# Four edits in the last attention layer: the next norm, the output rows, the row sums and the last 64 rows' product

## The chip, the cores and the metric

The kernel runs on one core of one Trainium2 chip. The metric is the device time of one launch in microseconds (us), less is better. The engines of a core are called PE (TensorE, matmuls; its weight loads are listed apart), DVE (VectorE), ACT (ScalarE), POOL (GpSimd) and SP, whose queue issues all loads and stores of this part of the kernel. Each engine runs its instructions in the order in which the program issued them and waits on semaphores for the others.

## The reference, cut to what matters

Four layers run on x (8 batches of 100 rows of 512 channels) with a context of 361 rows for each batch, all in fp32. The change is in the last layer alone: two cross-attentions, each behind a layer norm, and an MLP.

```python
def _cross_attention(q_in, kv_in, wq, bq, wk, bk, wv, bv, wo, bo, bias_k, bias_v):
    qh = (q_in @ wq + bq).reshape(b, q_len, H, K)            # 16 heads of 128
    kh, vh = kv_in @ wk + bk, kv_in @ wv + bv                # one more key and value
    ...                                                      # per head: bias_k, bias_v
    weights = softmax(einsum('bqhk,bthk->bhqt', qh, kh) / sqrt(K))
    ctx = einsum('bhqt,bthk->bqhk', weights, vh).reshape(b, q_len, H * K)
    return ctx @ wo + bo

h = layer_norm(x, ln1_scale, ln1_offset)
x = x + _cross_attention(h, context, ... first weights ...)
h = layer_norm(x, ln2_scale, ln2_offset)
x = x + _cross_attention(h, context, ... second weights ...)
h = layer_norm(x, ln_mlp_scale, ln_mlp_offset)
return x + gelu(h @ w_fc1 + b_fc1) @ w_fc2 + b_fc2
```

## The kernel before, in words

The last layer runs as four steps: attention 1 and 2, each for two halves of four batches (400 rows of x, 200 in `HN`). x itself lies in DRAM (`xd`): `take_rows` loads rows of it and `put_rows` stores them. A step has three parts.

*Queries* (`project_queries`). The normed rows stand in `hT`, turned (channels on partitions). `wq` is applied head by head, two heads at a time, as one 2x2 block product in seven multiplications instead of eight (`seven_products`), which needs sums of the weights' blocks (`left_sums`, on POOL) and of the tokens' blocks (`right_sums` into `hs`, four DVE instructions ahead of the first head pair). Each product is a matmul `pq`. Then `wk` is applied to the queries (`pk`), so that scores can be taken against the raw context: `qz` holds, per batch, 512 channels for 1600 rows (16 heads of 100). `some_keys` puts the `pk` of the head pair before between the products of this pair; in the first pair there is none before, and nothing is put there.

*Attention* (`attend`, once per batch). 1600 rows are 12 tiles of 128 (`NT`, `TR`) and 64 rows left over (`RR`). A tile pair's scores (`pair_of_scores`, 128x361 each in the banks `su` and `sl`) are again a block product in seven multiplications, with context sums `ts` once per batch and row sums `ss` once per pair, all on POOL. `softmax` follows on DVE and ACT, `turn_rows` turns the probabilities (`pt`, into `at`), and `block_with_context` multiplies four tiles by the context: weights are blocks of the context rows `cr` and their sums `cs`, with `at` moving, and the result overwrites `qz`. Products wait in the list `waiting`, and `meanwhile` takes parts of it, up to 256 rows' worth, between the products of a later pair: so PE's order is made. The 64 left rows of two batches are done together as one tile of 128: the scores (L1377) put the two batches' results in the two halves of a bank's partitions, and after the softmax `with_context` multiplies each batch's 64 rows: 4 channel blocks of 3 context blocks, each with weights `cr` 121x128 and 64 columns moving, 24 matmuls for the two batches. The results are channel by row, as `qz` has them.

*Outputs* (`project_outputs`). For each pair of heads: `wv` applied to `qz` (`pa`, L97 by its helper), the added key's part `u` (loaded from `pd`, L1443, then POOL), their sum `aT` (DVE, L1454), sums of `wo` (POOL) and the seven products `po` (L1416) of the pair before, which DVE adds to seven sums in SBUF, `acc` (L1425), of which three lie in the tile tag `oT` of the pool `big` and four in the tile `more` of the pool `l3_out`. The last pair ends with a few more adds (L1427). Then 16 transposes per step (L1466) turn the sums into rows, DVE adds them to x's rows (L1467) and `put_rows` stores these. `normalize` is called ahead of `project_outputs` and norms the rows of the *next* step (the other half, or after the second attention the MLP's first half): loads, `bn_stats`, `xhat` (L109), transposes (L128), and ACT's scale and offset into the next `hT`. Both loads of x's rows use the four buffers of tag `xin`.

Pools: `big` and `l3_2` stay for the layer, `l3_ctx` (context and its sums) is open in a step's queries and attention, `l3_out` in its outputs, in the same place. The MLP's first weights' second part is loaded into memory that `big` and others held (L1512), so that load waits for their last readers; the first part is loaded before the last outputs.

Of the kernel before, what the change touches and what calls it, by code (L numbers as in the profile page):

```python
# [10 lines left out]
F32 = mybir.dt.float32  # L11
# [45 lines left out]
def kernel(ctx: ExitStack, tc: tile.TileContext, d: dict, out: bass.AP):  # L57
# [1015 lines left out]
    with ExitStack() as es:  # L1073
# [85 lines left out]

        def project_queries(layer, hT, added):  # L1160
            ep, ahead = None, None
# [9 lines left out]

            b = [[hT[:, 2 * k : 2 * k + 2, n * HN : (n + 1) * HN] for n in range(2)] for k in range(2)]
            hs = big.tile([P, 4, 2, HN], F32, tag="oT", name="hs")
            hs = [hs[:, k] for k in range(4)]
            right_sums(nc.vector, b, hs)
            for h in range(0, NH, 2):
                wqs = [head_tile("wq", layer, h + m, "wa", [P, NC, P]) for m in range(2)]
                wks = [head_tile("wk", layer, h + m, "wb", [P, C]) for m in range(2)]
                a = [[w[:, 2 * k : 2 * k + 2, :] for k in range(2)] for w in wqs]
                s = p2.tile([P, 4, 2, TR], F32, tag="ss4", name="wqs").rearrange("p i k r -> p (i k r)")  # L1180
                s = [s[:, k * 2 * P : (k + 1) * 2 * P].rearrange("p (k m) -> p k m", k=2) for k in range(3)]
                left_sums(nc.gpsimd, a, s)
                banks = [ps.tile([P, 512], F32, tag=g, name=n) for g, n in (("z", "pq"), ("mm", "pq"))]
                tu = p2.tile([P, 3, HN], F32, tag="xhat", name="tu")
                if h == 10:
                    ep = added_scores(hT, er, *added)
# [23 lines left out]

        def attend(b, i, ep, pd, waiting, turning, pc, loaded):

# [4 lines left out]
            nc.sync.dma_start(out=cr, in_=d["ctxR"][b])  # L1217
            loaded.append((cT, cr))


# [7 lines left out]


            bs = [[cT[:, 2 * k : 2 * k + 2, j * SH : (j + 1) * SH] for j in range(2)] for k in range(2)]  # L1230
            ts_ = pc.tile([P, 4, 2, SH], F32, tag="ts", name="ts", bufs=1)
            nc.gpsimd.tensor_tensor(ts_[:, 0], bs[0][1], bs[0][0], ALU.subtract)
            nc.gpsimd.tensor_tensor(ts_[:, 1], bs[1][1], ts_[:, 0], ALU.subtract)  # L1233
            nc.gpsimd.tensor_tensor(ts_[:, 2], bs[1][1], bs[0][1], ALU.subtract)
            nc.gpsimd.tensor_tensor(ts_[:, 3], bs[1][0], ts_[:, 1], ALU.subtract)

            def sums(t):

# [7 lines left out]

            def with_context(i, cr, cs, at, r0):
                n = at.shape[-1]
                pz = ps.tile([P, 512], F32, tag="z", name="pz")
                pz = pz[:, : 2 * n].rearrange("p (c n) -> p c n", c=2)  # L1250
                for k, c in enumerate(cs):
                    mm_sum(
                        pz[:, k],
                        [
                            (cr[:m, kb, c * P : (c + 1) * P], at[:m, kb])
                            for kb, m in enumerate((KB, KB, S - 2 * KB))
                        ],
                    )
                evict(qz[:, i, cs[0] : cs[0] + 2, r0 : r0 + n], pz)

# [11 lines left out]
            def pair_of_scores(t):  # L1272
                rows, s = sums(t)
                banks = [ps.tile([P, 512], F32, tag=g, name=n)[:TR] for g, n in (("sc", "su"), ("mm", "sl"))]
                tu = p2.tile([P, 3, HN], F32, tag="xhat", name="tu")[:TR, :, :SH]

                def first():
# [7 lines left out]
                    tu, (first, meanwhile),  # L1285
                )
                return banks

            def block_with_context(at, r0):
# [5 lines left out]
                t = pc.tile([KB, 3, 2 * TR], F32, tag="bt", name="bt", bufs=1)  # L1295
                u1 = pc.tile([P, 2, 2 * TR], F32, tag="u1", name="u1", bufs=1)
                nc.gpsimd.tensor_tensor(t[:, 1], b[1][1], b[0][1], ALU.subtract)
# [18 lines left out]

                def second():
                    plus(u1, product([(cs[:, 1], t[:, 0])]), c12)
                    plus(c21, product([(cs[:, 2], t[:, 1])]), u1)

                def third_():
                    pz = product([(cs[:, 0], b[0][1]), (a[1][2][:third], b[2][1][:third])])
                    plus(c12, pz, u1)
                    plus(c22, pz, c21)
# [7 lines left out]
            def turn_rows(pr, at, parts):  # L1332
# [7 lines left out]
                for i, cr, part, r0 in parts:  # L1340
                    n = part.shape[-1]
                    nc.sync.dma_start(out=pd[i : i + 1, r0 : r0 + n], in_=part[S - 2 * KB : S + 1 - 2 * KB, 2])
                    if n == 4 * TR:
                        waiting.extend(block_with_context(part, r0))
                        continue
                    waiting.extend(
                        (lambda i=i, cr=cr, part=part, r0=r0, cs=cs: with_context(i, cr, cs, part, r0), n)
                        for cs in ((0, 1), (2, 3))
                    )

# [38 lines left out]

        def project_outputs(layer, half, pd, dv, po_):  # L1390
# [70 lines left out]
            oT = [[acc[1], acc[6]], [acc[5], acc[4]]]  # L1461
            for i, b in enumerate(bs):
                pt = ps.tile([P, 512], F32, tag="tp", name="pt")
# [3 lines left out]
                nc.vector.tensor_tensor(x[b], pt[:L, :], x[b], ALU.add)  # L1467
            put_rows(bs)

# [9 lines left out]
        steps = [(layer, half) for layer in (1, 2) for half in range(2)]  # L1479
        hT = third[3]  # L1480
        for n, (layer, half) in enumerate(steps):
# [3 lines left out]
            ep, late = project_queries(layer, hT, (wx, ch))  # L1485
            pd = dram.tile([HB, ROWS], F32, tag="pd", name="pd")
            waiting, turning = [(part, 2 * TR) for part in late], []
            loaded = []
            for i in range(HB):
                attend(half * HB + i, i, ep, pd, waiting, turning, pc, loaded)  # L1490
# [5 lines left out]
            if n == len(steps) - 1:  # L1496
                pw1 = ctx.enter_context(tc.tile_pool(name="mlp_w1", bufs=1, side="right"))
                w1 = [load(pw1, "L3_xattn_w_fc1", NC, C, f"fc1_{k}", lo=k * C) for k in range(2)]
            with tc.tile_pool(name="l3_out", bufs=2, side="right") as po_:
                hT = normalize(*(steps[n + 1] if n + 1 < len(steps) else ("_mlp", 0)), po_)  # L1500
                project_outputs(layer, half, pd, dv, po_)

# [229 lines left out]
```

## Time and profile before

| | |
|---|---|
| median of 3 runs | 2748.88 us (2748.11 to 2750.48) |
| the profiled execution | 2747.97 us, span 2745.9 us |
| mean granted PE clock | 0.983 |
| last layer's four steps | 833 us to 2568 us of the span |
| one step's queries, attention, outputs (second step) | 85, 263, 86 us |
| MLP | 2568 us to the end |
| PE busy, of the second step's 85, 263 and 86 us | 82.5, 261.6, 84.2 us |

The profile comes from one execution: a page with sums, and a trace that is read by line, by wait and by time. A line such as `PE pt L128 <- DVE xhat L109: 7.0, 8, 2.0` says that PE's instructions of line 128 on tile `pt` waited 7.0 us in all, 8 times, at the longest 2.0 us, for DVE's line 109. In the timeline, a row is a run of like instructions on one engine, with the start in the span, the length, and after the operation its tiles (out<-in) and shapes; for matmuls the weights' shape comes first and then the moving operand's.

### The profile page before, as it was taken

The numbers are of one execution on the slowest core, as the hardware profiler recorded it, in microseconds if no ns is written. First come the engines' busy times: TensorE is split into PE (matmuls) and PEld (weight loads), VectorE is DVE, ScalarE is ACT, GpSimd is POOL, SyncE is SP. The second block draws the span as 40 slices with busy tenths as digits, with TensorE's granted clock in tenths as the row PEclk, the third lists the DMA queues.
The fourth block names the chain that finished last, engine by engine and source line by source line (L and its number), as shares of the span: only waits on it lengthen the run. The fifth ranks groups of instructions, "written<-read, shape, count | busy, mean of one in ns | idle before, by whom it ended". The sixth has DMA issues, their size and how long they took to land.

```text
span 2745.9 us, 40332 instructions
## 1 busy us (share of the span) xinstructions
PE 2621.6 (95%) x14356; PEld 2093.8 (76%) x14356; DVE 1605.1 (58%) x3995; ACT 935.8 (34%) x2143; POOL 1042.8 (38%) x1362
## 2 busy tenths in 40 slices
PE   8999888888989999999999999999999999999999
PEld 5666466666666888877788877789887788886688
DVE  4788366877524656546556546555554655654743
ACT  5777334543321333310233330243331143331121
POOL 2000144532204445355345446344546334535212
PEclk9999889999999999999999999999999999999999
DMA  7432333354205100045200035400015510005400
GB/s 228 119 102 74 121 110 123 94 151 121 81 26 154 51 23 23 7 130 161 78 23 23 1 91 149 127 19 23 12 38 147 148 43 23 23 7 162 155 13 13
DMA packets 149682, 220.63 MB, mean 80 GB/s; under 512 B 45302, under 2 KB 78646, under 8 KB 149226
## 3 DMA queue, kind: packets, MB, share of 16 engines
q1 hardware_dynamic: 149482, 218.05, 27.5%
q8 instruction: 114, 1.87, 0.3%
q14 instruction: 86, 0.70, 0.1%
HBM read 207.48 MB, written 10.53 MB: 79 GB/s over the span
## 4 chain that ended last, share of the span: by engine, by line
PE 67%; POOL 4%; DVE 3%; DMA 2%; issue 1%; ACT 1%; SPq 0%; DVEq 0%; POOLq 0%; ACTq 0%
PE pz L97 18%; PE sl L97 9%; PE pk L1168 6%; PE su L97 5%; PE pq L97 5%; PE po L1416 5%; PE pa L97 5%; PE pp L97 3%; PE pu L97 3%; PE pt L1336 2%; PE pl L97 2%; DMA xin<-xd 1%; PE sc L1377 1%; PE sc L97 1%; POOL ss L1241 1%
## 5 line engine op out<-in xcount | busy, mean ns | idle before, releaser
L97 PE MATMUL pz<-at,cr 121*128 121x256 f32 (+1 forms) x960 | 255.3, 378 | 0.0
L751 POOL TENSOR_TENSOR st<-st,r 128x800 f32<-128x800 f32 x64 | 111.8, 1748 | 233.5 <-DVE st L745 195.3
L1311 DVE TENSOR_TENSOR qz<-pz,qz 128x512 f32<-128x512 f32 x192 | 131.9, 687 | 113.7 <-PE pz L97 105.8
L97 PEld LDWEIGHTS pz<-at,cr 121*128 121x128 f32 (+1 forms) x960 | 177.5, 189 | 21.0
L1168 PE MATMUL pk<-q,wb 128*128 128x400 f32 x512 | 189.9, 501 | 3.1 <-issue 3.1
L97 PE MATMUL pa<-qz,wa 128*128 128x400 f32 x512 | 178.2, 499 | 0.1
L97 PE MATMUL sl<-ts,ss 128*128 128x181 f32 x768 | 156.5, 325 | 3.7 <-POOL ts L1233 0.2
L97 PE MATMUL pz<-at,cs 121*128 121x256 f32 (+1 forms) x576 | 149.7, 380 | 0.0
L1241 POOL TENSOR_TENSOR ss<-qz 128x256 f32<-128x256 f32 x96 | 69.8, 727 | 207.1 <-PE su L97 118.4
L97 PEld LDWEIGHTS pa<-qz,wa 128*128 128x128 f32 x512 | 96.2, 190 | 64.9 <-DVE aT L1454 0.9
L1091 ACT COPY qz<-pk 128x400 f32<-128x400 f32 x128 | 63.0, 492 | 236.0 <-PE pk L1168 236.0
L1339 ACT COPY at<-pt 121x384 f32<-121x384 f32 x192 | 84.2, 480 | 159.2 <-PE pt L1336 94.1
L1358 ACT ACTIVATE pr<-su,nm 128x362 f32<-128x362 f32 x96 | 54.1, 564 | 239.4 <-DVE nm L1354 239.3
L97 PEld LDWEIGHTS sl<-ts,ss 128*128 128x128 f32 x768 | 118.2, 190 | 21.3 <-issue 7.1
L1168 PEld LDWEIGHTS pk<-q,wb 128*128 128x128 f32 x512 | 93.6, 190 | 50.5 <-ACT qz L1091 3.7
L350 PEld LDWEIGHTS pt<-ident,pr 115*121 115x121 f32 (+1 forms) x672 | 83.2, 185 | 56.5 <-ACT at L230 29.2
L745 DVE TENSOR_TENSOR_SCAN st<-wd,a 128x808 f32<-128x808 f32 x64 | 117.0, 1828 | 14.7 <-PE py L756 12.9
L1361 ACT ACTIVATE pr<-pr,ss 128x362 f32<-128x362 f32 x200 | 113.5, 595 | 31.7 <-DVE ss L1359 31.6
L342 ACT ACTIVATE pr<-pr,nm 115x361 f32<-115x361 f32 (+1 forms) x224 | 115.2, 592 | 10.4 <-DVE nm L338 10.4
L97 PEld LDWEIGHTS pz<-at,cs 121*128 121x128 f32 (+1 forms) x576 | 104.4, 189 | 13.7 <-issue 1.8
L338 DVE CUSTOM_DVE_ANT_0 pr<-sc,mask 115x361 f32<-115x361 f32 (+1 forms) x224 | 106.0, 530 | 11.0 <-PE sc L326 10.8
L350 PE MATMUL pt<-ident,pr 115*121 115x115 f32 (+1 forms) x672 | 99.9, 280 | 11.0 <-ACT at L230 5.4
(383 smaller groups left out, 6241.1 us busy)
## 6 DMA issues: line engine op xcount, KB each, us to landing
va<-vd SPq DMA_DIRECT2D x64, 404.0 KB
wa<-in_L_xattn_wq SPq DMA_DIRECT2D x64, 256.0 KB
wb<-in_L_xattn_wk SPq DMA_DIRECT2D x64, 256.0 KB
wa<-in_L_xattn_wv SPq DMA_DIRECT2D x64, 256.0 KB
wb<-in_L_xattn_wo SPq DMA_DIRECT2D x64, 256.0 KB
u<-pd SPq DMA_DIRECT2D x64, 200.0 KB
cr<-in_ctxR SPq DMA_DIRECT2D x16, 726.0 KB
cx<-in_ctxT SPq DMA_DIRECT2D x16, 722.0 KB
```

The costliest lines, as they stand in the source:

```text
L97: nc.tensor.matmul(dst, lhsT=lt, rhs=r, start=(i == 0), stop=(i == len(pairs) - 1))
L338: nc.vector.tensor_tensor_reduce(out=pr[:n], in0=sc[:n, :S], in1=mk[t][:n], scale=-1.0, scalar=FLT_MAX, op0=ALU.add, op1=ALU.min, accum_ou ...
L342: nc.scalar.activation(pr[:n], pr[:n], AF.Exp, bias=nm[:n], scale=-1.0)
L350: nc.tensor.transpose(pt[:KB, k * n : (k + 1) * n], pr[:n, lo : lo + KB], ident[:n, :n])
L745: nc.vector.tensor_tensor_scan(st.rearrange("p q b l -> p (q b l)"), wd.rearrange("p q t -> p (q t)"), a, 0.0, ALU.mult, ALU.add,)
L751: nc.gpsimd.tensor_tensor(st, st, rc.unsqueeze(1).to_broadcast([P, 4, UB, L]), ALU.mult)
L1168: nc.tensor.matmul(pk[:, :HT], lhsT=wk[:, c * P : (c + 1) * P], rhs=q, start=True, stop=True)
L1241: nc.gpsimd.tensor_tensor(ss_[:, 0], rows[1][0], rows[1][1], ALU.add)
L1311: nc.vector.tensor_tensor(dst, pz, other, ALU.add)
L1339: nc.scalar.copy(at, pt[:KB, : 3 * TR].rearrange("p (k r) -> p k r", r=TR))
L1361: nc.scalar.activation(pr[:, : S + 1], pr[:, : S + 1], AF.Copy, scale=ss)
L1416: nc.tensor.matmul(po[:, c], lhsT=left[k][:, c * P : (c + 1) * P], rhs=right[k], start=True, stop=True)
```

## The change

Four edits, all in the last layer:

1. The last 64 rows. `with_context` goes. `last_rows` has `at` as weights (64 columns) and all 512 channels of `cr` moving: three matmuls for each of the two batches, into the two halves of one bank's partitions. ACT copies the bank to SBUF, four transposes turn it back to channel by row, and two evictions write `qz`. It takes two places of 256 rows in `waiting`, where four of 64 were taken.
2. The next norm and the token sums are made inside the output part, ahead of the fourth head pair (`h == 6`), and so are the loads of the rows for the residual. All seven sums of `acc` lie in `l3_out`.
3. The transposes, adds and stores of a step's rows are called from the next step's queries, in the first head pair, at the two places where later pairs have `pk`; `l3_out` closes after the second. After the last step they follow the outputs as before.
4. The row sums `ss` of a pair are issued one pair sooner (`made`), and `ts` ahead of `cs`.

```diff
+        def token_blocks(hT):
+            b = [[hT[:, 2 * k : 2 * k + 2, n * HN : (n + 1) * HN] for n in range(2)] for k in range(2)]
+            hs = big.tile([P, 4, 2, HN], F32, tag="oT", name="hs")
...
+            right_sums(nc.vector, b, hs)
+            return b, hs
...
-        def project_queries(layer, hT, added):
+        def project_queries(layer, hT_all, hT, added, first_between):
...
-            right_sums(nc.vector, b, hs)
+            b, hs = hT
+            hT = hT_all
...
                 def some_keys(cs, ahead=ahead):
+                    if ahead is None:
+                        first_between(cs[0][0])
...
-            def with_context(i, cr, cs, at, r0):
...
+            def last_rows(at, crs):
+                held = []
+                def first():
+                    pz = ps.tile([P, 512], F32, tag="z", name="pl")
+                    for kb, m in enumerate((KB, KB, S - 2 * KB)):
+                        for q, cr in enumerate(crs):
+                            nc.tensor.matmul(
+                                pz[q * RR : (q + 1) * RR, :], lhsT=at[:m, kb, q * RR : (q + 1) * RR], rhs=cr[:m, kb, :],
+                                start=(kb == 0), stop=(kb == 2),
+                            )
+                    lr = pc.tile([P, 2, 2 * TR], F32, tag="u1", name="lr", bufs=1).rearrange("p i n -> p (i n)")
+                    nc.scalar.copy(lr, pz)
+                    held.append(lr)
+                def second():
+                    pz = ps.tile([P, 512], F32, tag="z", name="pl")
+                    for c in range(NC):
+                        nc.tensor.transpose(pz[:, c * P : (c + 1) * P], held[0][:, c * P : (c + 1) * P], ident)
+                    for q in range(2):
+                        evict(
+                            qz[:, i - 1 + q, :, NT * TR :],
+                            pz.rearrange("p (c r) -> p c r", c=NC)[:, :, q * RR : (q + 1) * RR],
+                        )
+                return [(part, 2 * TR) for part in (first, second)]
...
             def pair_of_scores(t):
-                rows, s = sums(t)
+                rows, s = made.pop((i, t)) if (i, t) in made else sums(i, t)
...
+                if t + 2 < NT:
+                    made[i, t + 2] = sums(i, t + 2)
+                elif i + 1 < HB:
+                    made[i + 1, 0] = sums(i + 1, 0)
...
-            acc = big.tile([P, 4, 2, HN], F32, tag="oT", name="acc")
-            more = po_.tile([P, 4, 2, HN], F32, tag="acc", name="more", bufs=1)
-            acc = [acc[:, 0], more[:, 0], acc[:, 1], acc[:, 2], more[:, 1], more[:, 2], more[:, 3]]
+            acc = po_.tile([P, 7, 2, HN], F32, tag="acc", name="acc", bufs=1)
+            acc = [acc[:, k] for k in range(7)]
...
-            take_rows(bs, po_, tag="xin", bufs=HB)
             ahead = None
             for h in range(0, NH, 2):
+                if h == 6:
+                    normalize_next()
+                    take_rows(bs, po_, tag="xin", bufs=HB)
...
-            for i, b in enumerate(bs):
+            def rows(i):
+                b = bs[i]
...
-            put_rows(bs)
+                put_rows([b])
+            return rows
...
+            def first_between(k):
+                if rows_of_last is not None:
+                    rows_of_last(2 * k)
+                    rows_of_last(2 * k + 1)
+                if k:
+                    at_outputs.close()
+            ep, late = project_queries(layer, hT, blocks_of_hT, (wx, ch), first_between)
...
+            def normalize_next():
+                nonlocal hT, blocks_of_hT
+                hT = normalize(*(("_mlp", 0) if last else steps[n + 1]), po_)
+                blocks_of_hT = None if last else token_blocks(hT)
+            rows_of_last = project_outputs(layer, half, pd, dv, po_, normalize_next)
+        for i in range(HB):
+            rows_of_last(i)
+        at_outputs.close()
```

More of the change, by code (lines that the diff above doesn't have):

```diff
@@ L1158, in right_sums @@
             eng.tensor_tensor(s[2], b[1][0], s[0], ALU.subtract)
-        def project_queries(layer, hT, added):
+        def token_blocks(hT):
+            b = [[hT[:, 2 * k : 2 * k + 2, n * HN : (n + 1) * HN] for n in range(2)] for k in range(2)]
+            hs = big.tile([P, 4, 2, HN], F32, tag="oT", name="hs")
+            hs = [hs[:, k] for k in range(4)]
+            right_sums(nc.vector, b, hs)
+            return b, hs
+        def project_queries(layer, hT_all, hT, added, first_between):
             ep, ahead = None, None
@@ L1169, in through_keys @@
                     evict(qz[:, :, c, h * L : (h + 1) * L], pk[:, :HT].rearrange("p (b l) -> p b l", l=L))
-            b = [[hT[:, 2 * k : 2 * k + 2, n * HN : (n + 1) * HN] for n in range(2)] for k in range(2)]
-            hs = big.tile([P, 4, 2, HN], F32, tag="oT", name="hs")
-            hs = [hs[:, k] for k in range(4)]
-            right_sums(nc.vector, b, hs)
+            b, hs = hT
+            hT = hT_all
             for h in range(0, NH, 2):
@@ L1209, in project_queries, with attend @@
             return ep, late
-        def attend(b, i, ep, pd, waiting, turning, pc, loaded):
+        def attend(b, i, ep, pd, waiting, turning, pc, loaded, made):
             cT = pc.tile([P, NC, S + 1], F32, tag="cT", name="cT")
@@ L1218, in attend @@
             loaded.append((cT, cr))
+            bs = [[cT[:, 2 * k : 2 * k + 2, j * SH : (j + 1) * SH] for j in range(2)] for k in range(2)]
+            ts_ = pc.tile([P, 4, 2, SH], F32, tag="ts", name="ts", bufs=1)
+            nc.gpsimd.tensor_tensor(ts_[:, 0], bs[0][1], bs[0][0], ALU.subtract)
+            nc.gpsimd.tensor_tensor(ts_[:, 1], bs[1][1], ts_[:, 0], ALU.subtract)
+            nc.gpsimd.tensor_tensor(ts_[:, 2], bs[1][1], bs[0][1], ALU.subtract)
+            nc.gpsimd.tensor_tensor(ts_[:, 3], bs[1][0], ts_[:, 1], ALU.subtract)
             cs = pc.tile([KB, 5, 2 * P], F32, tag="cs", name="cs", bufs=1)
@@ L1227, in attend, with sums @@
             nc.gpsimd.tensor_tensor(cs[:, 4], a[0][2], a[1][2], ALU.subtract)
[L1230 to L1237, printed above, removed]
+            def sums(i, t):
                 rows = [[qz[:, i, 2 * k : 2 * k + 2, r * TR : (r + 1) * TR] for k in range(2)] for r in (t, t + 1)]
@@ L1245, in sums @@
                 return rows, ss_
-            def with_context(i, cr, cs, at, r0):
[L1248 to L1259, printed above, removed]
+            def last_rows(at, crs):
[21 more added lines that the diff above has]
+                return [(part, 2 * TR) for part in (first, second)]
             def meanwhile():
@@ L1295, in block_with_context @@
                 t = pc.tile([KB, 3, 2 * TR], F32, tag="bt", name="bt", bufs=1)
-                u1 = pc.tile([P, 2, 2 * TR], F32, tag="u1", name="u1", bufs=1)
+                us = []
                 nc.gpsimd.tensor_tensor(t[:, 1], b[1][1], b[0][1], ALU.subtract)
@@ L1317, in second @@
                 def second():
+                    u1 = pc.tile([P, 2, 2 * TR], F32, tag="u1", name="u1", bufs=1)
+                    us.append(u1)
                     plus(u1, product([(cs[:, 1], t[:, 0])]), c12)
@@ L1322, in third_ @@
                     pz = product([(cs[:, 0], b[0][1]), (a[1][2][:third], b[2][1][:third])])
-                    plus(c12, pz, u1)
+                    plus(c12, pz, us[0])
                     plus(c22, pz, c21)
@@ L1344, in turn_rows @@
                         waiting.extend(block_with_context(part, r0))
[L1345 to L1349, printed above, removed]
+                if len(parts) == 2:
+                    waiting.extend(last_rows(at, [cr for _, cr, _, _ in parts]))
             def softmax(sc, e, at, parts):
@@ L1388, in attend, with project_outputs @@
                     softmax(sc, NT * HB + i // 2, at, parts)
-        def project_outputs(layer, half, pd, dv, po_):
-            acc = big.tile([P, 4, 2, HN], F32, tag="oT", name="acc")
-            more = po_.tile([P, 4, 2, HN], F32, tag="acc", name="more", bufs=1)
-            acc = [acc[:, 0], more[:, 0], acc[:, 1], acc[:, 2], more[:, 1], more[:, 2], more[:, 3]]
+        def project_outputs(layer, half, pd, dv, po_, normalize_next):
+            acc = po_.tile([P, 7, 2, HN], F32, tag="acc", name="acc", bufs=1)
+            acc = [acc[:, k] for k in range(7)]
             bo = [col(f"L3_xattn_bo{layer}", c) for c in range(NC)]
@@ L1480 @@
         hT = third[3]
+        blocks_of_hT = token_blocks(hT)
+        rows_of_last, at_outputs = None, ExitStack()
         for n, (layer, half) in enumerate(steps):
             wx, ch, dv = added[layer]
+            def first_between(k):
[5 more added lines that the diff above has]
+            ep, late = project_queries(layer, hT, blocks_of_hT, (wx, ch), first_between)
             at_right = ExitStack()
             pc = at_right.enter_context(tc.tile_pool(name="l3_ctx", bufs=2, side="right"))
-            ep, late = project_queries(layer, hT, (wx, ch))
             pd = dram.tile([HB, ROWS], F32, tag="pd", name="pd")
             waiting, turning = [(part, 2 * TR) for part in late], []
-            loaded = []
+            loaded, made = [], {}
             for i in range(HB):
-                attend(half * HB + i, i, ep, pd, waiting, turning, pc, loaded)
+                attend(half * HB + i, i, ep, pd, waiting, turning, pc, loaded, made)
             for part in turning:
@@ L1495 @@
             at_right.close()
-            if n == len(steps) - 1:
+            last = n == len(steps) - 1
+            if last:
                 pw1 = ctx.enter_context(tc.tile_pool(name="mlp_w1", bufs=1, side="right"))
                 w1 = [load(pw1, "L3_xattn_w_fc1", NC, C, f"fc1_{k}", lo=k * C) for k in range(2)]
-            with tc.tile_pool(name="l3_out", bufs=2, side="right") as po_:
-                hT = normalize(*(steps[n + 1] if n + 1 < len(steps) else ("_mlp", 0)), po_)
-                project_outputs(layer, half, pd, dv, po_)
+            at_outputs = ExitStack()
+            po_ = at_outputs.enter_context(tc.tile_pool(name="l3_out", bufs=2, side="right"))
+            def normalize_next():
[6 more added lines that the diff above has]
+        at_outputs.close()
     FF = 2048
```

## The prediction, made before the changed kernel was run

> **What bounds the kernel.** I read the page first: TensorE (PE) is busy 95% of the span, no other engine above 58% (weight loads, 76%, run beside matmuls).
>
> ```profile
> PE 2621.6 (95%) x14356; PEld 2093.8 (76%) x14356; DVE 1605.1 (58%) x3995; ACT 935.8 (34%) x2143; POOL 1042.8 (38%) x1362
> ```
>
> The change touches layer 3 alone, from 833 us on, so I then cut that stretch by stage (columns: stretch, its length, busy time and instructions of PE, of its weight loads, DVE, ACT, POOL, granted clock, DMA share, GB/s). These rows are an output part, a query part, an attention part, the last output part and the start of the MLP:
>
> ```profile
> 1180.00:1265.00 85.00, 83.04 (x373) 63.71 (x373) 44.07 (x83) 9.14 (x27) 58.60 (x88) 1.00 0.55 147
> 1265.00:1350.00 85.00, 82.46 (x362) 60.56 (x361) 51.31 (x115) 16.04 (x36) 29.99 (x44) 1.00 0.50 141
> 1350.00:1613.00 263.00, 261.62 (x1493) 232.87 (x1493) 152.00 (x411) 97.39 (x247) 120.41 (x170) 1.00 0.06 17
> ...
> 2480.00:2568.00 88.00, 83.79 (x371) 63.56 (x370) 44.26 (x81) 10.23 (x27) 52.78 (x79) 1.00 0.54 147
> 2568.00:2618.00 50.00, 47.01 (x162) 26.93 (x161) 42.52 (x90) 18.28 (x35) 5.27 (x5) 1.00 0.49 176
> ```
>
> The attention part is 99.5% PE: there only fewer or shorter passes help. At the seams PE idles 2 to 4 us a stage. The third view, PE's waits from 833 us to the end, says on what (total, times, longest):
>
> ```profile
> PE pt L128 <- DVE xhat L109: 7.0, 8, 2.0
> PE pq L97 <- DVE hs L1156: 5.6, 4, 3.1
> PE pk L1168 <- issue: 3.1, 3, 1.0
> PE pt L1466 <- DVE more L1427: 2.9, 4, 0.8
> PE pp L97 <- DMA fc<-in_L_xattn_w_fc: 2.1, 1, 2.1
> ...
> PE po L1416 <- DVE acc L1093: 1.7, 2, 1.4
> PE po L1416 <- DVE acc L1425: 1.5, 1, 1.5
> ```
>
> Fourth, PE's timeline in an attention part, where the last 64 rows' product runs (start, length with pipeline tail, then shapes; an fp32 matmul is two passes, each counted):
>
> ```profile
> 979.55 2.65 PE L1377 MATMUL sc<-cT,qz 128*64 128x361 f32 x16
> 982.13 1.99 PE L97 MATMUL pz<-bt,cs 121*128 121x256 f32 x8
> 983.96 0.82 PE L1336 MATMUL pt<-ident,pr 128*121 128x128 f32 x6
> 984.62 0.60 PE L97 MATMUL pz<-at,cs 121*128 121x256 f32 x2
> ...
> 989.99 1.90 PE L97 MATMUL pz<-at,cs 121*128 121x256 f32 x8
> 991.72 0.49 PE L1336 MATMUL pt<-ident,pr 128*121 128x128 f32 x3
> ...
> 996.08 2.56 PE L97 MATMUL pz<-last,cr 121*128 121x64 f32 x22
> 998.48 0.53 PE L97 MATMUL sl<-cT,qz 128*128 128x181 f32 x2
> ```
>
> I read a pass's price from one start to the next. A 256-column pass: (991.72 − 989.99) / 8 = 0.216, so 512 columns take 0.43. A 128-column transpose: (984.62 − 983.96) / 6 = 0.11. A 64-column pass: (998.48 − 996.08) / 22 = 0.109, hardly below that of 128 columns: these passes are bound by loading 128 weight columns, not by the 64 rows they serve. The first line is the precedent for the new form: 64-wide weights, the two batches' results in the two halves of PSUM's partitions, in turn. Singly, 16 passes of 361 columns would take 16 × 0.216 × 361 / 256 = 4.87 us; they took 982.13 − 979.55 = 2.58. So two passes, one per half, run side by side: 8 matmuls take 8.5 slots of 0.305.
>
> **The change part by part.** Sums are against the profiled run, 2747.97 us (span 2745.9 and 2.1 around it); the median, 2748.88, is 0.9 higher, which I add at the end.
>
> **Last 64 rows by rows** (8 batch pairs). Removed: 24 matmuls, 48 passes × 0.109 = 5.23 us a pair, and four evictions of 128x128 (0.27 to 0.29 each). Added: 6 matmuls, 12 passes of 512 columns at 0.43, one ACT copy of 128x512 (the like copy L1314: 0.59), 4 transposes × 0.11 = 0.44, two evictions of 256 columns. In the built order the six matmuls stand as one alone, four score matmuls, five together, four score matmuls, transposes. One alone has both passes in one half: 2 slots. Five in turn overlap all but the first and last pass: 6 slots. 8 × 0.43 + 0.44 = 3.88, gain 1.35 a pair, **10.8 in all**. Ends: no overlap, 12 × 0.43 + 0.44 = 5.60, a loss of 3.0 in all; full overlap, 6 slots, 3.02, a gain of 17.7. I take the order's count because the score line has this shape. The copy is queued behind two exponentials of the pair (0.56 each and 0.2 for reading the sum) and followed by the two normalisings that the next pt transposes need. Its cover is the second four score matmuls (1.24 us). Counted from the end of the first four (996.08), ACT's timeline has the exponentials start at 1.35 (997.43), so they end at 2.9; the five matmuls end at 2.6, the copy at 3.5, and the transposes are due at 2.6 + 1.24 = 3.8. With that cover gone the copy costs its 0.59 × 8 = 4.7. DVE and ACT (58% and 37% busy in this part) carry fewer evictions.
>
> A rule speaks against it. The Trainium skill, "TensorE: Matmul & The Clock Gate", Part 3 "Packing small matmuls", says that a weight load overlaps running matmuls only where the row group differs; here both halves use the same rows. In the score line (16 passes, 2.58 us) the loads are hidden, so the row disagrees with it. By the rule each of 12 loads of some 53 ns (its P/1.2, an estimate) would stand open: 0.64 a pair, and the sum would hold 5.1 less gain.
>
> **Next norm inside the output part** (4 steps). Its loads, bn_stats, rstd, xhat and transposes stand before the outputs now, where PE waits 7.0 us (L109) in eight waits, two a step. After, pa of six heads (48 passes of 400 columns, 0.216 × 400 / 256 = 0.34 each: 16 us) and po of two head pairs stand ahead of the transposes in PE's order, while DVE makes xhat, four times a step. I count the 7.0. In the last step PE also waits 1.7 + 1.5 for acc, which stand behind the MLP's norm on DVE; half of that, 1.6. I take **8.6**, with ends 0 (each wait moves to a new place: DVE, 44 of 85 us busy, now serves po's adds and the norm together) and 10.3 (all idle of four output parts: 1.96 + 1.85 + 2.31 + 4.21). Each step still issues four norm loads and four residual loads on SP and the same hT evictions; the residual loads use the norm's four buffers, so SP stands until xhat has been read, and wa, u and wb of later heads stand behind it.
>
> **Token sums, and last turnings among the next queries** (3 seams). Four DVE sums (some 0.5 each) move from the seam to the output part: three of the four hs waits, 5.6 − 3.1 = 2.5, go (the 3.1 is before the first step and stays). Two groups of eight turnings stand between the first head pairs' products; PE's first pk comes after 20 products and turnings, where q's eviction had been awaited: 3.1 goes. What is late next is the final adds: the first turning still waits for acc (0.7 to 0.8), so 2.9 stays. **5.0**, rounding 5.6 down for the new evictions' order; ends 0 and 8.5 (with the 2.9). The puts, and context loads behind them on SP, come some 4 us later; the context is used some 70 us after its load, the cover.
>
> **Row sums a pair sooner.** The same four POOL additions; POOL's order in the attention part and PE's waits on it come out as before. **0**; bounds 0 and the 0.2 of PE's one wait on L1233.
>
> **Start of the MLP.** fc's second load (L1512) had to wait until acc left the pool that it takes; acc is elsewhere now. The chain of waits there, by time:
>
> ```profile
> 2579.15 10.04 DMA xd<-xin
> ...
> 2589.46 4.99 DMA fc<-in_L_xattn_w_fc
> ...
> 2594.58 11.66 PE pp L97 x34
> ```
>
> The puts (10.04) share the DMA engines with that load; earlier, it frees them, and the 2.1 wait may go. But the built order puts the MLP's second xhat transposes after one matmul of fc's next part instead of 17: without a sooner xhat PE stands 32 passes of the 11.66, 11.0 us. **0** is taken between −11.0 and +2.1: near the good end, because the load should move by more than ten us, less what the order may cost.
>
> Sum: 10.8 + 8.6 + 5.0 = 24.4. 2748.0 − 24.4 + 0.9 = **2724.5**.
>
> **Rivals.** (1) The halves don't overlap, or the copy is late: the rows' product loses 3.0 in place of 10.8 gained: 2724.5 + 13.8 = 2738. For it: weight loads of 64 columns, which both halves bring in through the same rows, and the two exponentials ahead of the copy. Against: the score line. (2) PE stands at the MLP's transposes: 2724.5 + 11 = 2735.5. For it: the order; against: the load that goes early. (3) Fuller overlap (17.7) and every seam closed (10.3 + 8.5 + 2.1), 38.6 in all: 2710; against it the single first matmul. (4) Slower: SP's queue. The residual loads of a step wait for DVE's xhat reads, and loads of the next heads stand behind:
>
> ```profile
> 1191.14 2.23 SPq L1068 DMA_DIRECT2D xin<-xd  x4
> ```
>
> Before, this stood 2.2 us early on; later a head pair's loads are issued every 10 us, one pair ahead. Delay beyond some 10 us becomes PE idle, in four steps: from (24.4 + 5.5) / 4 = 7.5 us of idle a step, so some 17 us of standing, it is slower; at 8 a step, 2724.5 + 32 = 2756.5. Against: DVE is half idle there. That the change doesn't do what it says (no shorter waits, only moved) is the lower end of the seams: 2748.9 − 10.8 = 2738.
>
> **How the numbers follow.** Forecast 0.58, rival (1) and its like, the moved waits, 0.14, (2) 0.12, (3) 0.08, (4) 0.08. Under 0.2% (5.5 us) no measurement of this kernel tells from none: faster is below 2743.4. (1) and (2) alone stay below that, but together they reach 2749, no change: 0.05 for such sums. Faster 0.87, same 0.05, slower 0.08. The forecast's own range, ±8 for half the seams, is 2716 to 2733; to leave no more than 0.2 out I go to 2712 and 2740.
>
> **What would show it.** Right: in the attention parts, five 512-column matmuls in about 2.7 us and transposes without a wait for lr; each part some 2.5 us shorter; no wait of xhat's transposes on L109 nor of pk on issue; hs waited for once. Wrong: five matmuls in 4.3 us or more; PE waiting for lr; po or pa waiting for u, wa or wb in the output parts; pp or the MLP's xhat transposes waiting several us; or a lower granted clock than 1.00 in these rows.

## The result, and the profile after

The changed kernel takes 2724.98 us (median of 4 runs, 2722.49 to 2725.73) against 2749.68 us before (4 runs): a ratio of 0.9906, 95% interval 0.989 to 0.9922, 24.7 us less. Its profiled execution took 2724.63 us, with a span of 2722.8 us and a granted clock of 0.985.

The page's first line of the changed kernel:

```profile
PE 2609.8 (96%) x14100; PEld 2059.3 (76%) x14100; DVE 1601.2 (59%) x3987; ACT 939.2 (34%) x2143; POOL 1042.7 (38%) x1362
```

PE has 256 instructions less, 8 x (48 − 12 − 4) passes of the last rows' product, and only 11.8 us less of busy time: of the 24.7 us about half must have been idle time. The stretches of an attention part, the output part and the query part behind it (columns as before):

```profile
1341.30:1603.45 262.15, 260.78 (x1432) 225.05 (x1431) 151.96 (x409) 98.38 (x247) 120.68 (x170) 1.00 0.06 17
1603.45:1687.32 83.87, 83.09 (x369) 63.25 (x368) 45.88 (x85) 8.85 (x26) 58.77 (x87) 1.00 0.53 149
1687.32:1769.32 82.00, 81.70 (x363) 61.14 (x362) 49.04 (x111) 16.38 (x36) 29.64 (x43) 1.00 0.50 145
```

And PE's waits from 833 us to the end:

```profile
PE pt L128 <- DVE xhat L109: 2.5, 1, 2.5
PE pq L97 <- POOL cT L1222: 1.9, 1, 1.9
PE pz L97 <- POOL bt L1324: 1.8, 4, 0.5
PE po L1439 <- DVE acc L1093: 1.6, 2, 1.3
PE pt L1493 <- DVE acc L1450: 1.6, 3, 0.8
PE po L1439 <- DVE acc L1448: 1.4, 1, 1.4
```

Of the eight waits on xhat, 7.0 us, none is left in the output parts. The 2.5 us is a new place, the start of the MLP. The waits of `pk` are gone, and of hs's four only that of the first step (3.1) remains, which this stretch's edge cuts off.

For what follows I cut every trace at PE's first instruction of each part. Within one profile the four attention parts agree to 0.3 us, while whole runs of one kernel spread over 2.6 to 19 us, so parts are compared, not totals alone. The other parts repeat less well: in the nine builds whose seams between the steps wait alike (changed, e2 to e4, e6 to e10) the three pairs take 495.6 to 498.8, so a difference of under some 3 us in that column says nothing. The MLP is counted to the start of PE's last instruction. Sums in us, each from one profile:

| run | median | 4 attention parts | 3 pairs of output part and next queries | last output part | MLP |
|---|---|---|---|---|---|
| before | 2749.68 | 1054.1 | 509.8 | 88.2 | 173.7 |
| changed | 2724.98 | 1048.3 | 496.9 | 86.6 | 173.5 |
| e1 last rows alone | 2748.21 | 1048.1 | 515.6 | 87.6 | 173.8 |
| e2 all but the last rows | 2734.42 | 1054.1 | 497.5 | 85.1 | 174.9 |
| e3 six matmuls together | 2721.10 | 1039.3 | 496.2 | 85.0 | 176.7 |
| e4 full width | 2741.45 | 1058.6 | 495.6 | 85.9 | 175.3 |
| e5 norm at the start | 2736.76 | 1048.1 | 502.7 | 90.3 | 172.3 |
| e6 rows at the end | 2725.39 | 1048.1 | 496.5 | 85.0 | 175.3 |
| e7 token sums late | 2727.75 | 1048.1 | 497.6 | 84.5 | 175.2 |
| e8 e3 and rows' loads first | 2719.89 | 1039.3 | 497.8 | 85.1 | 175.2 |
| e9 e6 and e7 | 2723.93 | 1048.2 | 496.6 | 84.7 | 175.0 |
| e10 e8 and MLP's turning later | 2713.05 | 1039.3 | 498.8 | 85.2 | 170.7 |
| e11 e9, acc back in big | 2730.91 | 1048.3 | 503.6 | 84.8 | 173.2 |
| e12 before, acc in l3_out | 2741.68 | 1054.4 | 505.2 | 87.4 | 172.2 |

The time before the first changed instruction lies between 830.3 and 839.6 us in these fourteen profiles although it runs the same code: that is the spread of the totals, and 1.5 us of the two profiles' difference (833.5 and 832.0).

### The profile page after: what moved, and what is told of

It is laid out like the page before. It is cut to its first block, busy times and chain, and to the rows that moved or that the text cites. A ratio compares the mean times of both kernels' runs of the same rounds, so it can differ in the third digit from the quotient of the medians.

```text
span 2722.8 us, 39771 instructions
## 1 busy us (share of the span) xinstructions
PE 2609.8 (96%) x14100; PEld 2059.3 (76%) x14100; DVE 1601.2 (59%) x3987; ACT 939.2 (34%) x2143; POOL 1042.7 (38%) x1362
## 4 chain that ended last, share of the span: by engine, by line
PE 67%; POOL 4%; DVE 3%; DMA 2%; ACT 1%; issue 1%; SPq 0%; DVEq 0%; POOLq 0%; ACTq 0%
PE pz L97 16%; PE sl L97 9%; PE pk L1175 6%; PE su L97 6%; PE pq L97 5%; PE pa L97 5%; PE po L1439 5%; PE pp L97 3%; PE pu L97 3%; PE pt L1363 2%; PE pl L97 2%; PE pl L1262 1%; DMA xin<-xd 1%; PE sc L1401 1%; PE sc L97 1%
## 5 line engine op out<-in xcount | busy, mean ns | idle before, releaser
L97 PE MATMUL pz<-at,cr 121*128 121x256 f32 (+1 forms) x960 | 255.9, 378 | 0.0
L97 PEld LDWEIGHTS pz<-at,cr 121*128 121x128 f32 (+1 forms) x960 | 177.2, 189 | 20.8
L97 PE MATMUL pa<-qz,wa 128*128 128x400 f32 x512 | 178.7, 500 | 0.8 <-DVE aT L1479 0.8
L97 PE MATMUL sl<-ts,ss 128*128 128x181 f32 x768 | 156.7, 326 | 3.8 <-POOL ts L1231 0.5
L97 PE MATMUL pz<-at,cs 121*128 121x256 f32 (+1 forms) x576 | 149.7, 380 | 0.0
L97 PEld LDWEIGHTS pa<-qz,wa 128*128 128x128 f32 x512 | 95.7, 190 | 65.9 <-DVE aT L1479 2.3
L97 PEld LDWEIGHTS sl<-ts,ss 128*128 128x128 f32 x768 | 118.4, 190 | 21.9 <-issue 7.1
L1448 DVE TENSOR_TENSOR acc<-po,acc 128x400 f32<-128x400 f32 x196 | 111.4, 572 | 15.1 <-PE po L1439 0.5
L97 PEld LDWEIGHTS pz<-at,cs 121*128 121x128 f32 (+1 forms) x576 | 104.4, 189 | 13.7 <-issue 1.8
```

Of the source, the lines that this page charges most:

```text
L97: nc.tensor.matmul(dst, lhsT=lt, rhs=r, start=(i == 0), stop=(i == len(pairs) - 1))
L1448: nc.vector.tensor_tensor(acc[k], po, acc[k], ALU.add)
```

## The experiments

**The last 64 rows: e1 to e4.** The attention parts fell by 5.8 us where the prediction had 10.8. PE's timeline around one pair in the changed kernel:

```profile
990.16 0.78 PE L97 MATMUL su<-ts,ss 128*128 128x181 f32 x4
990.87 1.07 PE L1262 MATMUL pl<-cr,last 121*64 121x512 f32 x2
991.87 0.88 PE L97 MATMUL sl<-ts,qz 128*128 128x181 f32 x4
992.59 0.78 PE L97 MATMUL su<-cT,ss 128*128 128x181 f32 x4
993.30 2.79 PE L1262 MATMUL pl<-cr,last 121*64 121x512 f32 x10
996.02 0.88 PE L97 MATMUL sl<-cT,qz 128*128 128x181 f32 x4
996.74 0.78 PE L97 MATMUL su<-cT,qz 128*128 128x181 f32 x4
997.35 0.60 PE L1273 MATMUL pl<-ident,lr 128*128 128x128 f32 x4
```

Ten passes from 993.30 to 996.02: 2.72 for six slots of 0.43 (2.58), so the halves overlap and the count of slots was right. But the four score passes ahead of either group take 0.71 (990.16 to 990.87, 992.59 to 993.30) and four others 0.61 (996.74 to 997.35); those behind the second group take 0.72; the lone matmul takes 1.00 in place of 0.86, and the ten passes hold 0.14 more than their slots. In the trace's single rows the first 64-wide weights' load starts together with its pass, 0.09 late; inside the group loads run beside passes, and the passes of two neighbouring matmuls start 0.01 us apart (993.297 and 993.304). A change to 64-wide weights and back to 128-wide ones is called a round trip below; the expectations call its edges seams. e1 has this edit alone, e2 all but this edit:

```diff
 # e1, in the kernel before; e2 the other way, in the changed kernel
-    waiting.extend((lambda ...: with_context(i, cr, cs, part, r0), n) for cs in ((0, 1), (2, 3)))
+    waiting.extend(last_rows(at, [cr for _, cr, _, _ in parts]))
```

> The kernel before with only the last 64 rows' product by rows. Theory (the seams): each change between weights of 128 and of 64 columns costs PE some 0.1 us, since the next weights are not loaded beside the running pass, and each group of the new matmuls has one such change on each side and a longer first pass; the trace of the changed kernel has 0.8 us less per batch pair, so the four attention parts together get some 6 us shorter and the time falls by 6, to about 2743. Rival (the slots alone, as predicted): 1.35 us a pair, 10.8 us, 2738, and the changed kernel loses the other 5 in its attention parts to something else of the change, the sooner row sums for one.

> The changed kernel with the last 64 rows' product as before (24 matmuls of 64 columns a pair); the rest of the change stays. Theory: attention parts go back to 263.5 us each, the time rises by 6 to about 2731, and the seams' gain (outputs 8, queries 6 to 7 us) stays whole. Rival: the time rises by 10.8, to 2736.

Both bear the theory out by their parts: 1048.1 with this edit alone, 1054.1 without it, to 0.2 us the values of the two kernels: 6.0 us, 0.75 a pair. The sooner row sums, which e1 lacks and e2 has, change nothing. By its total e1 seems to have gained nothing (2748.21, ratio 0.9987, 0.9971 to 1.0004): its output parts are 1.7 to 2.5 us longer, for a reason shown further down. e2 is 2734.42, ratio 0.9936 (0.9911 to 0.9962).

e3 puts an order edge on the six matmuls:

```diff
+                    with tc.issue_after(last_mm[0].ins):     # the last score product's matmul
                     for kb, m in enumerate((KB, KB, S - 2 * KB)):
```

> The changed kernel with an order edge on PE, so that the six matmuls of a pair stand together, behind the last score product, in place of one and five. Slots alone: one slot of 0.43 and two of four changes of weights' width less, 0.77 us a pair, 6 us in all, 2719. Against it: the single matmul stood where the next score product waited for DVE (sl<-su,tu is done some 1.4 us after the start of the pair's fourth product), so PE should now wait some 0.9 us there for DVE in each pair; then the attention parts stay within 0.5 us of the changed kernel's 262.1 and the time is 2725 again.

Neither: the attention parts fell by 8.9 us more. PE's timeline there (two or three lines more in the file, so L99 is L97, and L130 below L128):

```profile
998.91 0.78 PE L99 MATMUL su<-ts,ss 128*128 128x181 f32 x4
999.53 0.78 PE L99 MATMUL sl<-cT,qz 128*128 128x181 f32 x4
1000.14 0.47 PE L99 MATMUL su<-cT,qz 128*128 128x181 f32 x2
1000.45 0.82 PE L99 MATMUL sl<-ts,qz 128*128 128x181 f32 x4
1001.11 0.78 PE L99 MATMUL su<-cT,ss 128*128 128x181 f32 x4
1001.81 2.80 PE L1265 MATMUL pl<-cr,last 121*64 121x512 f32 x12
1004.54 0.57 PE L99 MATMUL su<-cT,qz 128*128 128x181 f32 x2
```

The wait for DVE that the lone matmul had filled is filled by score products of the next pair, which the scheduler (the step of the build that puts each engine's instructions in order) drew forward. And twelve passes take 2.73, six slots: two neighbouring matmuls of different halves run wholly side by side, both passes, not one pass apart as I had counted. One and five made 2 + 6 slots because an odd one is left over in each. So e3 saves two slots (0.86) and one of the two round trips, 1.1 us a pair in all.

e4 uses all 128 columns as weights, one bank for each batch, 12 slots and no change of width; half of each bank is not used, and ACT copies the other half:

```diff
-  nc.tensor.matmul(pz[q * RR : (q + 1) * RR, :], lhsT=at[:m, kb, q * RR : (q + 1) * RR], rhs=cr[:m, kb, :], ...)
+  mm_sum(pz, [(at[:m, kb, :], cr[:m, kb, :]) for kb, m in enumerate((KB, KB, S - 2 * KB))])   # for each q
```

> The changed kernel with all 128 columns of the turned probabilities as weights for each of the two batches' contexts, into a bank for each, of which half the rows are used: no change of weights' width, no pass beside another, 12 passes of 0.43 a pair. Theory (the seams cost some 0.6 us a pair): 1.72 us more for four more slots, 0.6 less, so 1.0 to 1.1 a pair, attention parts 2.1 us longer than the changed kernel's 262.1 and the time 2733. Rival (the seams cost nothing and the missing gain is elsewhere): 1.72 a pair, attention parts 3.4 longer, 2739.

```profile
997.42 0.78 PE L97 MATMUL su<-ts,ss 128*128 128x181 f32 x4
998.03 1.02 PE L97 MATMUL pl<-cr,last 121*128 121x512 f32 x2
998.90 0.88 PE L97 MATMUL sl<-ts,qz 128*128 128x181 f32 x4
999.62 0.78 PE L97 MATMUL su<-cT,ss 128*128 128x181 f32 x4
1000.23 4.46 PE L97 MATMUL pl<-cr,last 121*128 121x512 f32 x10
1004.53 0.78 PE L97 MATMUL sl<-cT,qz 128*128 128x181 f32 x4
```

Here the four score passes ahead take 0.61, the two passes 0.87, the ten 4.30: no seam there, and no overlap (the 0.72 behind the lone matmul is there without a change of width, so it is no seam). The parts are 10.3 us longer than the changed kernel's, 1.29 a pair; four slots more are 1.72, so the seams cost 0.43 a pair, less than the 0.58 that the rows above add up to (0.10 twice, 0.13, 0.14, 0.11), and far from nothing.

**The seams between the steps: e5 to e7, e9, e11, e12.** e5 calls the norm ahead of the outputs again (`if h == 0` for `if h == 6`).

> The changed kernel with the next norm and the residual loads ahead of the first head pair of the output part again (the token sums too); all else stays. Theory: xhat's transposes stand again where they come before xhat is made, two waits per step, 1.8 to 2.0 us each step in the first three, and the output parts are 1.2 to 3.2 us longer each, 7 to 8 us in all, 2732. Rival (the shorter output parts come from elsewhere, such as the sums acc being all in one pool or the rows' turning being gone from their end): under 3 us in all. If PE's idle of 2 us is followed by a lower granted clock, as in a run of the second kind above (0.98 over an output part, four passes of pa in 2.75 us instead of 1.53), an output part may be up to 2 us longer still.

xhat's waits are back (7.4 us in nine waits, 1.2 of it at the MLP), the three pairs are 5.8 us longer, the last output part 3.7 (of which some 1.7 is a lowered clock, see the end): the theory, though the time, 2736.76, is longer than its 2732. e6 turns the rows behind the outputs again, e7 makes the token sums at the start of the queries:

```diff
 # e6, in the loop over the steps
-        for i in range(HB):
-            rows_of_last(i)
-        at_outputs.close()
+            for i in range(HB):
+                rows_of_last(i)
+            at_outputs.close()
+            rows_of_last, at_outputs = None, ExitStack()
 # e7, in project_queries; normalize_next makes no token sums then
-            b, hs = hT
             hT = hT_all
+            b, hs = token_blocks(hT)
```

> The changed kernel with the turning, adding and storing of a step's rows right behind its outputs in all steps, and nothing between the first head pair's products of the next queries. Theory: the wait of pk on q's eviction (1.0 us) comes back at each of three seams, and the wait for the final adds (0.2 to 0.6 in the changed kernel) is 0.7 to 0.8 again; the three query parts are 1.4 us longer each (part of that shows as the output part's end), 4 to 5 us in all, 2729. Rival (the queries' gain comes from the token sums alone): under 1 us.

> The changed kernel with the token sums made at the start of the queries again, the turning still between the first products. Theory: the four DVE sums stand behind the final adds and the residual adds, and the first hs product comes after two transposes of tokens' own products; the wait L1156 of 0.8 us comes back at three seams, 2.5 us in all, 2727. Rival: the turnings between the products cover it, 0.

e6 fell: its three pairs are 0.4 us shorter than the changed kernel's, `pk` waits for nothing. e7 fell too, by parts: its pairs are 0.7 us longer in all where 2.5 was expected, and hs is waited for in the first step alone. Its median, 2727.75, looks like the theory's 2727, but in the profile 1.7 us is a longer MLP, for the reason shown at the end. I took them for two covers of one gap and undid both (e9).

> The changed kernel with both edits at the seam undone: token sums at the start of the queries, and the rows' turning right behind the outputs. Each alone undone left the sum of an output part and the query part behind it as it was (165.4 to 165.9 us in the changed kernel, 164.8 to 166.1 with the turning undone, 165.2 to 166.5 with the sums undone). Theory: either covers the same waits, and only with both undone do hs L1156 (0.8) and pk on issue (1.0) come back at three seams; the sum rises by about 2 us at each of three seams, to 167.5, 6 us in all, 2731. Rival: the waits had gone for another reason (acc in one pool, the norm inside the outputs) and nothing rises.

That theory fell as well: 496.6 us, 2723.93. The two edits that I had held for the gain bring nothing that these sums can show. The rows of hT (ACT) and hs (DVE) in e9, whose program writes hs down behind the outputs, for the second step:

```profile
1202.34 5.33 ACT L130 ACTIVATE hT<-pt,pv 128x100 f32<-128x100 f32 x16 [9.71 <-PE pt L128]
1207.05 0.58 DVE L1155 TENSOR_TENSOR hs<-hT 128x400 f32<-128x400 f32 x1
1207.73 0.80 DVE L1156 TENSOR_TENSOR hs<-hT,hs 128x400 f32<-128x400 f32 x1
```

and in the kernel before, where hT is done at 1197.1, with the last of the final adds:

```profile
1267.80 0.57 DVE L1427 TENSOR_TENSOR more<-more,acc 128x400 f32<-128x400 f32 x1
1269.48 0.56 DVE L1155 TENSOR_TENSOR hs<-hT 128x400 f32<-128x400 f32 x1
1271.16 0.56 DVE L1156 TENSOR_TENSOR hs<-hT,hs 128x400 f32<-128x400 f32 x1
```

hs runs 60 us sooner, as soon as hT is there (1207.67). What held it before was room: hs and three of the sums of acc share the tile tag `oT`, one buffer, so hs had to wait for the last reader of these three, the final adds at the seam (L1427). With acc moved to l3_out nothing holds it, wherever it is written down: an engine's order is not simply that of kernel.py's lines, the scheduler makes it. e11 takes e9 and puts acc back; e12 takes the kernel before and moves acc alone:

```diff
-            acc = big.tile([P, 4, 2, HN], F32, tag="oT", name="acc")
-            more = po_.tile([P, 4, 2, HN], F32, tag="acc", name="more", bufs=1)
-            acc = [acc[:, 0], more[:, 0], acc[:, 1], acc[:, 2], more[:, 1], more[:, 2], more[:, 3]]
+            acc = po_.tile([P, 7, 2, HN], F32, tag="acc", name="acc", bufs=1)
+            acc = [acc[:, k] for k in range(7)]
```

> The run with both edits at the seam undone (three pairs of output and query part 496.6 us together, as in the changed kernel), and three of the seven sums of acc back in the tile tag oT, which the token sums hs use too. Theory: what took the waits at the seam away was neither edit but the room: hs may only be written when acc's last readers are done, and in the run with acc elsewhere the program's order has the four hs sums in the output part although they are written down behind it. So hs L1156 (0.8) and pk on issue (1.0) come back at three seams, the three pairs are 503 us, 2730; and the MLP's weights' second part is late again, PE waits for it and not for xhat. Rival: nothing rises, the norm inside the outputs did it all.

> The kernel before with one edit, two lines: all seven sums of acc in the pool l3_out; the norm ahead of the outputs, the turning behind them, the last 64 rows as before. Theory as in the run beside it: hs is made in the output part, hs L1156 waits once (3.1) instead of four times, pk on issue not at all, the three pairs of output and query part fall from 509.8 by some 6 to 503 to 504, 2743; xhat's waits of 7 us stay. Rival: the waits stay, 2749.

PE's waits in e11:

```profile
PE pq L97 <- DVE hs L1156: 5.5, 4, 3.1
PE pk L1175 <- issue: 3.1, 3, 1.0
...
PE pp L97 <- DMA fc<-in_L_xattn_w_fc: 2.0, 1, 2.0
```

and in e12:

```profile
PE pt L128 <- DVE xhat L109: 8.2, 9, 2.0
PE pq L97 <- DVE hs L1156: 2.9, 1, 2.9
```

In e11 all four waits of hs, those of `pk` and that for fc are back, to a tenth of a us, and the pairs are 503.6. In e12 they are gone but for the first step's wait on hs, each of the three query parts is 2.8 us shorter than before (81.9, 81.5 and 82.0 for 84.7, 84.3 and 84.8), and two lines give a quarter of the whole change, 6.6 of 24.7 us: 2741.68, ratio 0.9971 (0.9957 to 0.9984). Two of e12's output parts are 1.8 and 2.9 us longer, as e1's are; see below.

**The start of the MLP: e8, e10.** In the changed kernel the second part of the weights comes early, and PE waits for xhat of the second half of rows instead (2.5). These rows are stored (landed at 2555.1), then loaded, behind two more parts of weights:

```profile
2551.64 3.41 DMA xd<-xin
...
2557.57 9.53 DMA xin<-xd
```

e8 is e3 with `take_rows(range(HB, B), p1)` ahead of the loads of these weights.

> The changed kernel with the six matmuls of the last rows together, and the loads of the MLP's second half of rows ahead of the loads of the third and fourth part of its first weights on SP. Theory: attention parts 259.8 us as in the run with the six together (six matmuls in 2.73 us are six slots of 0.43, each two matmuls wholly side by side, where one and five take eight), 9 us less than the changed kernel; the rows' loads share the DMA engines with less and land some 4 us sooner, so that PE's 2.5 us at the MLP's xhat transposes goes, and with it a lowered clock behind it; 2713. Rival: the third weights' part comes too late then and PE waits for it instead, 2716.

```profile
2559.42 0.90 PE L130 MATMUL pt<-ident,xhat 100*128 100x100 f32 x4 [2.85 <-issue]
2560.11 1.58 PE L99 MATMUL pp<-hT,fc 128*128 128x400 f32 x2
```

The first half held (1039.3), the second fell, and the rival with it: the loads came sooner, but so did the transposes in PE's order, behind 48 passes of `pp` in place of 66, and PE waits 2.85 us for xhat (the view says issue; DVE's first xhat there ends at 2559.2). e10 moves them back, by drawing the norm's generator at later steps of the loop:

```diff
-                    next(norm, None)
+                    for _ in range((1, 0, 0, 0, 1, 2, 2, 0)[j]):
+                        next(norm, None)
```

> The run with the six matmuls together and the rows' loads first, and in addition the transposes of the MLP's second half of rows placed behind the fifth to seventh of the eight steps of its first product, in place of the second to fifth. Theory: xhat is ready some 21 us after the MLP's start (PE waited 2.85 us for it, and the passes behind that ran at half pace, 1.58 us for two in place of 0.9), and 80 passes, 27 us, now stand ahead of it, so the wait and the slow passes go: MLP 171 us in place of 173.5 to 176.7, 2714 or less. Rival: the second half's own product then waits for hT and its sums on POOL, and the MLP is 174 us again.

```profile
2543.55 24.35 PE L99 MATMUL pp<-hT,fc 128*128 128x400 f32 x72
2567.73 0.51 PE L130 MATMUL pt<-ident,xhat 100*128 100x100 f32 x4
```

No wait for xhat is left; the MLP falls by 4.5 us from e8, the 2.85 of idle time and 1.7 that the end of this text explains, and the kernel takes 2713.05 us, ratio 0.9868 to the kernel before (0.9845 to 0.989). It is the fastest of all.

## Why the prediction came out where it did

- *Sum.* 24.4 was forecast, 24.7 measured between medians; the profiled runs differ by 23.3, of which 1.5 us lie ahead of all changed code and 1.0 in the first step's queries, where the work is the same (the clock was lowered for 6.8 us there in the profile of before, and not in the other). So the parts that the change touches gave some 21, 3 to 4 less than forecast, and the agreement of 2724.5 with 2725.0 is closer than the terms deserve: it is luck.
- *Last 64 rows, 10.8; measured 5.8 to 6.0.* The mis-sized term of the sum: an attention part is 1.5 us shorter, not 2.5. Eight slots were right, but by luck: the passes run in pairs side by side and an odd matmul is left over in each group (e3), not shifted by one pass as I had it. What was left out are the changes of weights' width, two round trips in each of eight pairs, 0.43 a pair by e4 and 0.58 by the timeline; 0.62 a pair was missing, so up to 0.2 a pair stays open. The price of 2.58 for 16 passes in the scores' line held such a round trip (2.58 for eight slots of 0.305, 2.44): I read it as half a slot of overlap lost. For the same reason the end "full overlap, six slots" was a real one: e3 reached the six slots, and with one round trip left a gain of 14.8 of its 17.7 us.
- *The rule on weight loads.* The Trainium skill, "TensorE: Matmul & The Clock Gate", Part 3 "Packing small matmuls", by its line on what overlaps would have exposed every load: 12 a pair. Its price in the prediction, 0.64 a pair, is close to the 0.62 that was missing, but not for its reason: within a group the loads stay hidden (12 passes in 2.73 us in e3), and what costs are the edges, where 64-wide weights follow 128-wide ones or the reverse.
- *Next norm inside the outputs, 8.6; measured 6.2 in the three pairs* (e11 against before) *and 1.6 in the last output part* (88.2 to 86.6; 84.5 to 85.9 in e2 to e4 and e6 to e11). Right in place and nearly in size; of the waits for acc in the last part, of which half (1.6) was to go, 2.7 of 3.2 us stayed. SP's queue, the slower rival, did nothing: `pa` waits 0.8 us in two waits, and for DVE.
- *Token sums and turnings, 5.0; measured 6.7* (e11 against the changed kernel). The waits that I named went, and some of the third, on the final adds. The cause I gave was wrong: neither the call's place (e7) nor the turnings between the products (e6, e9) did it, but acc's move (e11, e12), which I had costed only for the MLP.
- *Row sums, 0*: right (e1, e2).
- *MLP, 0 between −11 and +2.1; measured 0.2.* The wait of 2.1 for fc went and one of 2.5 for xhat came, as rival (2) had it, at a quarter of its price. The 0.2 is partly luck: behind such an idle (2.3 to 2.9 us) seven other profiles show a lowered clock and an MLP 1.4 to 3.2 us longer than the changed kernel's.

## What to carry to other kernels

Before a stall is put down to where an instruction is written, ask which buffer it writes and who reads that last: here two lines that gave a tile its own room did what two rearrangements were thought to do, and the scheduler found the place by itself. Passes that share the array paid at the edges of their group here, so keep them in one group, with as many matmuls for the one half as for the other. A change of many edits can meet its forecast with two of its terms wrong, one in size and one in cause, so undo them one by one, and in pairs, and compare parts of the trace rather than totals.

## What the runs showed that I had not expected

An idle of about 2 us on PE can cost twice. In e1 PE waits for xhat as in the kernel before, and then:

```profile
1192.86 0.56 PE L128 MATMUL pt<-ident,xhat 100*128 100x100 f32 x4 [1.79 <-DVE xhat L109]
...
1194.00 2.75 PE L97 MATMUL pa<-qz,wa 128*128 128x400 f32 x4
```

Four passes take 2.75 us there and 1.53 in the profiled run before. Windows of 3.41 us around the idle give the granted clock, the third column from the end, for before:

```profile
1187.48:1190.89 3.41, 1.91 (x6) 0.76 (x4) 1.09 (x5) 0.30 (x1) 2.55 (x5) 1.00 0.78 195
1190.89:1194.31 3.42, 2.96 (x18) 2.14 (x19) 2.33 (x5) 2.54 (x8) 1.81 (x2) 1.00 0.51 122
```

and for e1:

```profile
1190.76:1194.17 3.41, 1.43 (x10) 0.94 (x10) 2.23 (x4) 0.71 (x3) 2.72 (x4) 1.00 0.71 148
1194.17:1197.58 3.41, 3.41 (x9) 1.99 (x9) 1.12 (x2) 2.12 (x8) 0.95 (x3) 0.50 0.65 199
```

The same wait, 1.8 us, was followed by a full clock in one execution and by half of it, for 3.41 us, in another. The traces show what the two differ in. In the clock records of all fourteen profiles a lowered clock is 0.50 and, but for the one at a program's end, lasts 3.41 us or two to four times that, and within one profile all such stretches begin on one grid of 3.41 us; the windows above are steps of that grid. e1's idle (1191.07 to 1192.86) lies in one step; that of before (1189.39 to 1191.17) is cut by a step's edge into 1.50 and 0.28. In the last layer and the MLP (from 845 us to 20 us before the end of the span), thirteen steps at full clock were followed by a lowered one, and PE was idle for 1.89 to 2.50 us of each; of the some 7600 others a single one (2.00, e1 at 2593.6) was idle for more than 1.81. So it looks as if the idle time within one step decides; where the steps' edges fall differs from profile to profile. No run tested that.

At half the clock a step loses up to 1.7 us. It explains e1's output parts (1.7, 2.5 and 1.7 us longer, one lowered step in each, none in its fourth) and the two of e12 (one each), and fits the MLP, which is longer than the changed kernel's by 1.4 to 1.9 us in e2, e4 and e6 to e9 (one lowered step behind 2.3 to 2.9 us of idle) and by 3.2 in e3 (two). In the changed kernel's profile the 2.5 us are cut into 1.40 and 1.08, and the clock stays; in e10 without the idle the MLP is the shortest. So the end of a wait can bring more than the list of waits shows, and in a single execution it may not. The Trainium skill ("TensorE: Matmul & The Clock Gate", Part 1) puts such a drop behind an idle window of some 3.4 us; the step's length agrees, but here steps that were idle for 1.9 to 2.5 us were enough.
